# Decoding two edge counts per 16 bit word, and moving one strip's node update into layer 1

## The chip, the cores and the metric

The kernel runs on one core of a Trainium2 chip. The metric is the device time in microseconds of one execution of the whole program; lower is better. Times inside an execution come from a profile of one execution on the chip, counted from the start of its span. The engines are called PE or TensorE (matrix products), DVE or VectorE (elementwise), ACT or ScalarE (activation functions and copies), POOL or GpSimd (small elementwise work) and SP (which only issues transfers here).

## The reference

Two graph layers over 3327 nodes with 64 features and a sparse 0/1 adjacency matrix, each behind a layer norm and a relu, each with a residual addition:

```python
# layer 0: h = relu(layernorm(x)); x = x + L0(h, adj)
left, right = x_t @ w_att[:D, 0], x_t @ w_att[D:, 0]        # x_t = logmap0(h)
adj_att = sigmoid(left[:, None] + right[None, :] + b_att) * adj
x_local = logmap(h[:, None, :], h[None, :, :], c)           # all pairs of nodes
support_t = einsum('ij,ijd->id', adj_att, x_local)
x = x + proj(expmap(h, support_t, c), c)
# layer 1: h = relu(layernorm(x)); x = x + L1(h, adj)
support = h @ weight
rank = cumsum(adj != 0, axis=1); deg = rank[:, -1:]
k = minimum(deg, 100); pos = rank - (deg - k)
w = (adj != 0) * where(pos > 0, 0.5 ** (k - pos), 0)
x = x + w @ support + bias
```

So an edge's weight in layer 1 is two to the power of minus the number of edges behind it in its row, and zero from the hundredth on. Layer 1 needs, for every pair of nodes, a small count; layer 0 reads the same adjacency matrix, so the counts are made there.

## The kernel before, in words

The 3327 nodes are padded to 26 blocks of 128 (`NP` = 3328). The input matrix is given transposed. Layer 0 goes over four **strips** of output nodes (`STRIPS`: blocks 0 to 7, 8 to 15, 16 to 21, 22 to 25), called strips 0 to 3 here; strip 2 is the second but last and strip 3 the last. Each strip goes over all 26 blocks of neighbours in **rounds** (one block in strips 0 to 2, two in the last). A round loads a piece of the matrix, makes a mask (L620), the pairwise products on TensorE (L670, L671), two gelu activations (L857, L858), the attention factor (L653), two combining operations on DVE (L658, L663), and adds to a sum in PSUM (L680, `total`).

In every round a matmul with a triangular matrix counts edges into PSUM (`count`, L631 and L632), and `read` takes the counts out, on ScalarE (L642) or on DVE (L644, L646) by a fixed share (`ON_ACT`). The count is written as one byte into `behind_lo` or `behind_hi`. It is made so that the byte is what the exponent of a bf16 number needs: multiplied by 128, that is shifted by seven bits, it is the bit pattern of the weight. For the blocks 12 to 15 (`JD`) `read` multiplies at once and writes 16 bit weights (`weight_of`); for the other blocks the byte is multiplied in layer 1 (`decode`, L1285 on ScalarE and L1287 on DVE, in turn: 11 each).

After each strip its sum is copied out (`strip_out`, L1157), transposed (`turn`, L1165) and handed to the **node update** (`post`): a long chain of small operations per node which ends in the new x (`x_sb`, L1126 and L1128), its layer norm (L1131 to L1144) and `s2`, the relu of it as two fp16 parts (L1147, L1149). For strips 0 to 2 (`hidden`) its small operations run on POOL and its large ones on DVE; for the last strip all run on DVE, except that the inverse square root is taken with a power on POOL (L1044 with `nhalf`). `post` is a generator: `yield` numbers are prices, and the loop around it (`advance`) lets it run for a certain sum of prices per round (`PORTIONS`) or per block of layer 1 (`LAST` = 8). `LATER` ends a turn, `ACT` asks for an operation of ScalarE, which is issued at the next turn (`asked_of_act`). When several stages are in the list `stages`, they share a turn's sum, the first in the list first. `after(time)` spreads the small operations: it waits ceil(time / `ROUND[k + 1]`) turns for a hidden strip.

The order of PE, DVE and ScalarE instructions is as written (`IN_ORDER`); POOL's order comes from the scheduler. POOL's last operations are, in this order: strip 2's small ones, the addition of the bias to strip 2's part of x (L1304, 128x384), strip 2's root for the layer norm, then three powers for the last strip with one more bias addition (128x256) among them.

**Layer 1** goes over the neighbour blocks in the order `JD` first, then 0 to 11, then 16 to 21, and last 22 to 25, whose `s2` come last. It keeps `LEAD` = 4 blocks decoded ahead in seven buffers `wt`. For each block TensorE adds seven matmuls (L1299), one for each chunk of 512 output columns (the last has 256), into seven PSUM tiles `pw`:

```python
for i, j in enumerate(order):
    for jn in every[: i + 1 + LEAD]:
        if jn not in weights:
            weights[jn] = decode(jn)
    asked_of_act()
    advance(LAST)
    for n in range(len(chunks)):
        add(j, weights[j], n)
```

The last four blocks are then added chunk by chunk. After each chunk its tile is copied out (L1342 on DVE, L1340 on ScalarE), multiplied by the weight matrix (L1328), added to x (L1330) and stored (L1332).

Of the kernel before, what the change touches and what calls it, by code (L numbers as in the profile page):

```python
# [22 lines left out]
P = 128  # L23
# [14 lines left out]

PORTIONS, LAST = (2, 4, 4, 8), 8
BIG, LATER, ACT = 4, 99, 100  # L40
ROUND = (3.5, 3.5, 2.8, 1.9)

LEAD = 4

GSTRIPS = [(0, 7), (7, 7), (14, 6), (20, 6)]
GFMAX = 7 * P
# [35 lines left out]
def halves(n):  # L82
    return [(a, min(a + 512, n)) for a in range(0, n, 512)]
# [363 lines left out]
def fast(ctx, tc, x, adj_t, r, w_att, b_att, weight, bias, out, flag):  # L447
# [76 lines left out]
    def wide(t, n):  # L524
        return t[:, :, None].to_broadcast([P, n, D])
# [96 lines left out]
    def count(n, j):  # L622
# [9 lines left out]
            T.matmul(S.pc[:, f0:f1], cb, now[:, f0:f1], start=S.first, stop=True, skip_group_check=True)  # L632
        S.before, S.first = now, False

    def read(n, j, on_act=None):
        k, lo, hi = rounds[n]
        S = strips[k]
        kept = behind(j)[:, S.i0 : S.i0 + S.F]
        num, den = ON_ACT[k]
        i = NB - 1 - j  # L640
        if on_act or (on_act is None and i * num // den != (i + 1) * num // den):
            A.activation(kept, S.pc[:, : S.F], AF.Relu, scale=128.0 if j in JD else 1.0)  # L642
        elif j in JD:
# [284 lines left out]
    def last_of_ahead():  # L928

        V.tensor_scalar(balm, bal, MIN_NORM, None, op0=ALU.max)  # L930
        V.reciprocal(sk, balm)
        yield
        G.tensor_scalar(w2s, w2, 2.0**27 / HS, None, op0=ALU.mult)
        G.tensor_scalar(ih, babs, 2 / WA, None, op0=ALU.mult)
        G.tensor_mul(su, nrm, balm)
        G.tensor_mul(sv, bal, su)
        G.tensor_scalar(sk, sk, sqc, None, op0=ALU.mult)
        G.tensor_scalar(maxnorm, absr, 1.0 - EPS_BALL, None, op0=ALU.mult)
        G.tensor_mul(c2_c, c_c, c_c)
        G.tensor_scalar(m2c, c_c, -2.0, None, op0=ALU.mult)  # L940
        G.tensor_scalar(p2c, c_c, 2.0, None, op0=ALU.mult)
        ahead.close()

        behind_of["lo"] = ctx.enter_context(tc.tile_pool(name="lo", bufs=1, side="right", reuse_waits="tile")).tile(
            [P, JD.start, NP], U8, name="behind_lo")
        yield


    def range_steps():
        t1 = post_pool.tile([P, NB], F32, name="st1")  # L950
        V.tensor_mul(t1, nrm, node)
# [40 lines left out]
    def post(agg, k):  # L992
# [48 lines left out]
        def after(time):  # L1041

            for do, args, kwargs in asked_of_w:
                do(*args, **kwargs)  # L1044
# [123 lines left out]
    def per_node(k, pa):  # L1168
        nb = STRIPS[k][1]
        agg = post_pool.tile([P, nb, D + 1], F32, name="agg_last" if k + 1 == len(STRIPS) else "agg")  # L1170
        for c in range(0, nb, 4):
            m = min(4, nb - c)
            to, of = agg[:, c : c + m], pa[:, c * P : c * P + m * (D + 1)].rearrange("p (b d) -> p b d", b=m)
            if c == 0:
                V.tensor_copy(to, of)
            else:
                A.copy(to, of)
        return post(agg, k)
# [5 lines left out]
    def advance(portions):  # L1184
        for stage in stages:
            while portions > 0 and not stage.asked:
                portion = next(stage.portions, LATER)
                stage.asked = portion == ACT
                if portion >= LATER:
                    break  # L1190
                portions -= portion
# [78 lines left out]

    late = STRIPS[-1][0]
    order = [*JD, *range(JD.start), *range(JD.stop, late)]
    chunks = halves(NP)
    with tc.tile_pool(name="l1", bufs=2, reuse_waits="tile") as l1, tc.manual_schedule(engines=IN_ORDER):
        decoded = 0

        def decode(j):

            nonlocal decoded
            if j in JD:  # L1280
                return behind(j)
            wt = l1.tile([P, NP], U16, name="wt", bufs=7)
            decoded += 1
            if decoded % 2:
                A.activation(wt, behind(j), AF.Copy, scale=128.0)  # L1285
            else:
                V.tensor_scalar(wt, behind(j), 128.0, None, op0=ALU.mult)  # L1287
# [7 lines left out]
        pw = [l1_ps.tile([P, f1 - f0], F32, name=f"pw{n}") for n, (f0, f1) in enumerate(chunks)]  # L1295

        def add(j, wt, n):
            f0, f1 = chunks[n]
            T.matmul(pw[n], s2[:, j].rearrange("p c d -> p (c d)"), wt[:, f0:f1].bitcast(BF16),  # L1299
                     start=j == order[0], stop=j == NB - 1)  # L1300

        def bias(b0, nb):
            xb = x_sb[:, b0 : b0 + nb]
            G.tensor_add(xb, xb, bias_b[:, None, :].to_broadcast([P, nb, D]))  # L1304
# [4 lines that stand above are left out]
                    weights[jn] = decode(jn)  # L1309
            asked_of_act()  # L1310
            advance(LAST)
            for n in range(len(chunks)):
                add(j, weights[j], n)
            if i % 4 == 3 and i < STRIPS[-2][0]:
                bias(i - 3, 4)
        finish()
        bias(STRIPS[-2][0], late - STRIPS[-2][0])
        bias(late, NB - late)
        for j in range(late, NB):
            if j not in weights:  # L1320
                weights[j] = decode(j)
        ow = [l1.tile([P, 512], F32, name="ow", bufs=4)[:, : f1 - f0] for f0, f1 in chunks]

        def close(n):
            f0, f1 = chunks[n]
            b0, nb = f0 // P, (f1 - f0) // P
            for b in range(nb):
                T.matmul(pw[n][:, b * D : (b + 1) * D], ow[n][:, b * P : (b + 1) * P], w2s, start=True, stop=True)  # L1328
            o = l1.tile([P, 4, D], F32, name="o", bufs=4)
            V.tensor_add(o[:, :nb], pw[n][:, : nb * D].rearrange("p (b d) -> p b d", d=D), x_sb[:, b0 : b0 + nb])  # L1330
            full = nb if b0 + nb < NB else nb - 1
            nc.sync.dma_start(out[f0 : f0 + full * P, :].rearrange("(b p) d -> p b d", p=P), o[:, :full])  # L1332
            if full < nb:
                nc.scalar.dma_start(out[f0 + full * P : N, :], o[: N - f0 - full * P, full])
# [12 lines left out]


@with_exitstack
# [49 lines left out]
```

## Time and profile before

| | |
|---|---|
| median of 3 runs | 418.17 us (416.35 to 418.49) |
| profiled execution, its own time | 418.25 us |
| profiled execution, span | 416.4 us |
| busy PE, DVE, ACT, POOL | 361.1, 373.1, 364.8, 124.0 us |
| last GELU of layer 0 ends (L858) | 354.89 us |
| sum of the last strip copied out (agg_last, L1175) | 360.46 us |
| last strip's s done (L1149) | 395.04 us |
| first matmul with all late blocks decoded (L1299) | 396.89 us |

The table's clock times are of the profiled execution, counted from the start of the span. A row of a profile names the line, the engine, the operation, the tile written and the tiles read, with partitions x elements and type. Busy time is how long an engine had an instruction running; idle time before an instruction is given with what released it. In the chain of waits each step is followed back from the last instruction to what it waited for.

### The profile page before, as it was taken

What the parts mean: (1) busy time and instruction counts of PE and PEld (TensorE: products, weight loads), DVE (VectorE), ACT (ScalarE), POOL (GpSimd) and SP (SyncE); (2) the same over time, 40 slices, a digit from 0 to 9 for tenths busy, and PEclk for the clock granted to TensorE, in tenths of its full rate; (3) what the DMA queues carried; (4) which work ended last, traced back from release to release, by engine and by line L of the source; (5) the groups of instructions that cost most, each with busy time, mean ns of one, the idle gap of its engine ahead of it and who ended that gap; (6) DMA issues with size and microseconds to landing.
All of it is one profiled execution on the core that took longest, in us unless ns stands there. A gap on an engine that the chain in (4) does not pass through costs nothing.

```text
span 416.4 us, 4699 instructions
## 1 busy us (share of the span) xinstructions
PE 361.1 (87%) x1436; PEld 154.4 (37%) x1460; DVE 373.1 (90%) x546; ACT 364.8 (88%) x411; POOL 124.0 (30%) x240
## 2 busy tenths in 40 slices
PE   0088999999997999999997999999777999899793
PEld 0063333333333333333333444444332333344352
DVE  4999799999999899999999798899989899898841
ACT  3589999999998899999999899999996999788810
POOL 8154200000000263930250163801405183452400
PEclk9998999999999899999999899999898999999987
DMA  7315544545466534554437255454643420000012
GB/s 218 123 40 143 161 148 147 158 145 161 146 186 181 152 107 148 153 151 109 145 113 178 94 153 151 119 146 128 186 117 104 114 87 0 2 0 0 2 25 65
DMA packets 23298, 48.99 MB, mean 118 GB/s; under 512 B 8789, under 2 KB 9245, under 8 KB 23265
## 3 DMA queue, kind: packets, MB, share of 16 engines
q1 hardware_dynamic: 20993, 47.66, 39.2%
q10 hardware_dynamic: 1808, 0.46, 0.6%
q0 software_dynamic: 464, 0.49, 0.5%
q8 instruction: 13, 0.21, 0.2%
q14 instruction: 20, 0.16, 0.1%
HBM read 46.40 MB, written 0.87 MB: 114 GB/s over the span
## 4 chain that ended last, share of the span: by engine, by line
DVE 33%; ACT 27%; PE 24%; issue 10%; POOL 3%; DMA 1%; DVEq 0%; POOLq 0%; ACTq 0%
DVE sg L663 9%; PE po L680 9%; ACT sg L653 8%; DVE sg L658 8%; ACT pq L857 8%; ACT pq L858 3%; DVE wt L1287 3%; PE pq L670 3%; PE pq L671 3%; DVE behind_lo L646 3%; PE pc L632 2%; PE pc L631 2%; ACT behind_lo L642 2%; ACT behind_hi L642 2%; PE pw L1299 2%
## 5 line engine op out<-in xcount | busy, mean ns | idle before, releaser
L680 PE MATMUL po<-sg,hw 128*65 128x512 f32 (+1 forms) x364 | 164.5, 576 | 0.5 <-DVE st L972 0.4
L663 DVE SCALAR_TENSOR_TENSOR sg<-pq,sg 128x1024 f32<-128x1024 f32 (+1 forms) x91 | 103.4, 1137 | 6.7 <-ACT pq L858 5.9
L658 DVE SCALAR_TENSOR_TENSOR sg<-sg,ad 128x1024 f32<-128x1024 f32 (+1 forms) x91 | 103.8, 1141 | 0.3
L653 ACT ACTIVATE sg<-left_b,right 128x1024 f32<-128x1024 f32 (+2 forms) x103 | 99.5, 979 | 0.0
L857 ACT ACTIVATE pq<-pq 128x1024 f32<-128x1024 f32 (+1 forms) x91 | 87.1, 957 | 3.5 <-PE pq L671 3.2
L858 ACT ACTIVATE pq<-pq 128x1024 f32<-128x1024 f32 (+1 forms) x91 | 86.2, 947 | 2.9
L680 PEld LDWEIGHTS po<-sg,hw 128*65 128x65 f32 x364 | 50.4, 141 | 71.3 <-issue 57.5
L631 PE MATMUL pc<-mask,ca 128*128 128x512 bf16 (+1 forms) x170 | 62.1, 365 | 11.1 <-DVE behind_hi L646 3.9
L670 PE MATMUL pq<-iu,ju 71*128 71x512 f16 (+1 forms) x182 | 68.2, 375 | 2.4 <-ACT jz L794 1.0
L671 PE MATMUL pq<-iz,jz 128*128 128x512 f16 (+1 forms) x182 | 67.2, 376 | 0.0
L632 PE MATMUL pc<-mask,cb 128*128 128x512 bf16 (+1 forms) x168 | 60.1, 368 | 2.2 <-ACT behind_lo L642 1.7
L620 DVE TENSOR_SCALAR mask<-ad 128x1024 bf16<-128x1024 f32 (+1 forms) x91 | 58.6, 645 | 0.0
L1044 POOL TENSOR_TENSOR dots<-dots,ih 128x8 f32<-128x8 f32 (+1 forms) x3 | 2.2, 720 | 134.3 <-DVE dots L1064 134.3
L1299 PE MATMUL pw<-wt,s 128*128 128x512 bf16 (+1 forms) x150 | 33.6, 374 | 4.3 <-DVE s L1149 2.2
L632 PEld LDWEIGHTS <-cb 128*128 128x128 bf16 x182 | 17.9, 98 | 51.7 <-issue 39.8
L631 PEld LDWEIGHTS <-ca 128*128 128x128 bf16 x175 | 17.3, 99 | 29.9 <-issue 17.8
L670 PEld LDWEIGHTS <-ju 71*128 71x128 f16 x182 | 18.1, 99 | 24.2 <-DVE sg L663 5.8
L1299 PEld LDWEIGHTS <-s 128*128 128x128 f16 x182 | 18.0, 100 | 23.6 <-issue 4.2
L642 ACT ACTIVATE behind_hi<-pc 128x1024 uint8<-128x1024 f32 (+2 forms) x25 | 21.8, 872 | 5.3 <-remote 3.3
L671 PEld LDWEIGHTS <-jz 128*128 128x128 f16 x182 | 18.2, 100 | 19.7 <-issue 3.3
L1304 POOL TENSOR_TENSOR x_sb<-x_sb,bias_b 128x256 f32<-128x256 f32 (+1 forms) x6 | 9.9, 1657 | 51.6 <-DVE w L1133 46.0
L642 ACT ACTIVATE behind_lo<-pc 128x1024 uint8<-128x1024 f32 (+2 forms) x29 | 24.9, 859 | 0.0
(313 smaller groups left out, 369.0 us busy)
## 6 DMA issues: line engine op xcount, KB each, us to landing
ad<-in_adj_t SPq DMA_DIRECT2D x65, 512.0 KB, 3.7
ad<-in_adj_t SPq DMA_DIRECT2D x26, 384.0 KB, 3.2
out<-o SPq DMA_DIRECT2D x6, 128.0 KB, 1.9
left_b<-left_d SPq DMA_DIRECT2D x1, 512.0 KB, 4.6
x_sb<-in_x ACTq DMA_DIRECT2D x1, 416.0 KB, 5.6
x_sb<-in_x SPq DMA_DIRECT2D x1, 416.0 KB
left_b<-left_d SPq DMA_DIRECT2D x1, 384.0 KB
jz<-iz POOLq DMA_DIRECT2D x2, 128.0 KB, 2.6
```

Of the source, the lines that this page charges most:

```text
L631: T.matmul(S.pc[:, f0:f1], ca, S.before[:, f0:f1], start=False, stop=True, skip_group_check=True)
L632: T.matmul(S.pc[:, f0:f1], cb, now[:, f0:f1], start=S.first, stop=True, skip_group_check=True)
L642: A.activation(kept, S.pc[:, : S.F], AF.Relu, scale=128.0 if j in JD else 1.0)
L653: A.activation(part(n, sg, j), S.left[:, : S.F], AF.Tanh, bias=right[:, j : j + 1], scale=0.5)
L658: V.scalar_tensor_tensor(sg, sg, 1.0, ad_of.pop(n)[:, :w], op0=ALU.add, op1=ALU.mult)
L663: V.scalar_tensor_tensor(sg, pq_of.pop(n)[:, :w], WD, sg, op0=ALU.add, op1=ALU.mult)
L670: T.matmul(part(n, pq, j, f0, f1), ju[:KB, j, :], S.iu[:, f0:f1], start=True, stop=False)
L671: T.matmul(part(n, pq, j, f0, f1), jz[:, j, :], S.iz[:, f0:f1], start=False, stop=True)
L680: T.matmul(S.po[: D + 1, f0:f1], hw[:, j, :], part(n, sg_of[n], j, f0, f1), start=j == NB - 1, stop=j == 0)
L857: A.activation(pq, pq, AF.Gelu, scale=-WG / QS)
L858: A.activation(pq, pq, AF.Gelu, scale=WH)
L1299: T.matmul(pw[n], s2[:, j].rearrange("p c d -> p (c d)"), wt[:, f0:f1].bitcast(BF16), start=j == order[0], stop=j == NB - 1)
```

## The change

Five things change together.

1. In layer 1 `decode` writes its weights **by parity**: the 1664 even columns first, then the 1664 odd ones. On DVE it takes two bytes as one 16 bit word: one operation keeps the low byte and shifts it left by seven, one keeps the high byte and shifts it right by one. On ScalarE it is still one activation, which reads every second byte. The two engines still decode in turn.
2. `read` writes the 16 bit weights of blocks 12 to 15 by parity too, so it reads every second word of the PSUM tile.
3. The chunks of layer 1 are now (q, r): the 512 even or odd columns of 1024; the last 256 columns stay together. The copies of the tiles put even and odd columns back in order in a tile of 1024, and the closing operations run for two tiles at a time.
4. The update of strip 2 stops ahead of its change of x until layer 1 has begun (the list `tail` is then filled). Its six operations of 128x384 (new x and the centred x of the layer norm) are issued there, in the first turns, ahead of the last strip's. It is finished at the latest when its own block is due.
5. In layer 1 `after` counts turns of 1.5 us instead of 1.9; the six microseconds that remain for strip 2 are four turns with either.

The core of the diff:

```diff
-ROUND = (3.5, 3.5, 2.8, 1.9)
+ROUND, STEP = (3.5, 3.5, 2.8, 1.9), 1.5
+ACT_DECODES = 2
...
+    def by_parity(t):
+        return t.rearrange("p (r k) -> p r k", r=2)
     def read(n, j, on_act=None):
...
+        of = S.pc[:, : S.F]
+        if j in JD:
+            kept = by_parity(weight_of[:, j - JD.start])[:, :, S.i0 // 2 : (S.i0 + S.F) // 2]
+            of = of.rearrange("p (k r) -> p r k", r=2)
         if on_act or (on_act is None and i * num // den != (i + 1) * num // den):
-            A.activation(kept, S.pc[:, : S.F], AF.Relu, scale=128.0 if j in JD else 1.0)
+            A.activation(kept, of, AF.Relu, scale=128.0 if j in JD else 1.0)
         elif j in JD:
-            V.tensor_scalar(kept, S.pc[:, : S.F], 0.0, 128.0, op0=ALU.max, op1=ALU.mult)
+            V.tensor_scalar(kept, of, 0.0, 128.0, op0=ALU.max, op1=ALU.mult)
...
-                yield from [LATER] * math.ceil(time / ROUND[k + 1])
+                yield from [LATER] * math.ceil(time / (STEP if tail else ROUND[k + 1]))
...
         yield from after(16)
+        while k + 2 == len(STRIPS) and not tail:
+            yield LATER
         V.tensor_mul(w, hs, wide(of_end[:, 0], nb))
...
-    def finish():
-        for stage in stages:
-            for _ in stage.portions:
+    def finish(left=0):
+        while len(stages) > left:
+            for _ in stages.pop(0).portions:
                 pass
-        stages.clear()
...
-    chunks = halves(NP)
+    chunks = [(q, r) for q in range(3) for r in range(2)] + [(3, None)]
+    widths = [512] * 6 + [256]
...
-            if decoded % 2:
-                A.activation(wt, behind(j), AF.Copy, scale=128.0)
+            to = by_parity(wt)
+            if decoded % ACT_DECODES == 1:
+                A.activation(to, behind(j).rearrange("p (k r) -> p r k", r=2), AF.Copy, scale=128.0)
             else:
-                V.tensor_scalar(wt, behind(j), 128.0, None, op0=ALU.mult)
+                pairs_of = behind(j).bitcast(U16)
+                V.tensor_scalar(to[:, 0], pairs_of, 0xFF, 7, op0=ALU.bitwise_and, op1=ALU.logical_shift_left)
+                V.tensor_scalar(to[:, 1], pairs_of, 0xFF00, 1, op0=ALU.bitwise_and, op1=ALU.logical_shift_right)
             return wt
...
+        tail.append(True)
         stages.append(Stage(per_node(len(STRIPS) - 1, pa)))
...
         def add(j, wt, n):
-            f0, f1 = chunks[n]
-            T.matmul(pw[n], s2[:, j].rearrange("p c d -> p (c d)"), wt[:, f0:f1].bitcast(BF16),
+            q, r = chunks[n]
+            w = by_parity(wt.bitcast(BF16))[:, :, 512 * q : min(512 * q + 512, NP // 2)]
+            T.matmul(pw[n], s2[:, j].rearrange("p c d -> p (c d)"), w if r is None else w[:, r],
                      start=j == order[0], stop=j == NB - 1)
...
             advance(LAST)
+            if j == STRIPS[-2][0]:
+                finish(1)
...
+        def copied(n):
+            q, r = chunks[n]
+            to = kept_of[q].rearrange("p (k r) -> p r k", r=2)
+            if r is None:
+                V.tensor_copy(to, by_parity(pw[n]))
+            elif r == 0:
+                V.tensor_copy(to[:, 0], pw[n])
+            else:
+                A.copy(to[:, 1], pw[n])
...
         for n in range(len(chunks)):
             for j in range(late, NB):
                 add(j, weights[j], n)
-            if n % 2:
-                A.copy(ow[n], pw[n])
-            else:
-                V.tensor_copy(ow[n], pw[n])
-            if n > 1:
-                close(n - 2)
-        close(len(chunks) - 2)
-        close(len(chunks) - 1)
+            copied(n)
+            if n > 0 and n % 2 == 0:
+                close(n // 2 - 1)
+        close(3)
```

More of the change, by code (lines that the diff above doesn't have):

```diff
@@ L1197, in asked_of_act @@
                 stage.asked = False
-    def finish():
-        for stage in stages:
-            for _ in stage.portions:
+    def finish(left=0):
+        while len(stages) > left:
+            for _ in stages.pop(0).portions:
                 pass
-        stages.clear()
+    tail = []
     stages, rest_of_ahead = [Stage(range_steps())], last_of_ahead()
@@ L1294, in fast @@
         l1_ps = ctx.enter_context(tc.tile_pool(name="l1_ps", bufs=1, space=PSUM, reuse_waits="tile"))
-        pw = [l1_ps.tile([P, f1 - f0], F32, name=f"pw{n}") for n, (f0, f1) in enumerate(chunks)]
+        pw = [l1_ps.tile([P, f], F32, name=f"pw{n}") for n, f in enumerate(widths)]
         def add(j, wt, n):
-            f0, f1 = chunks[n]
-            T.matmul(pw[n], s2[:, j].rearrange("p c d -> p (c d)"), wt[:, f0:f1].bitcast(BF16),
+            q, r = chunks[n]
+            w = by_parity(wt.bitcast(BF16))[:, :, 512 * q : min(512 * q + 512, NP // 2)]
+            T.matmul(pw[n], s2[:, j].rearrange("p c d -> p (c d)"), w if r is None else w[:, r],
                      start=j == order[0], stop=j == NB - 1)
@@ L1321, in fast, with close @@
                 weights[j] = decode(j)
[L1322 to L1334, printed above, removed]
+        kept_of = [l1.tile([P, min(NP - 1024 * q, 1024)], F32, name="ow" if q < 3 else "ow_last", bufs=2 if q < 3 else 1)
+                   for q in range(4)]
+        def copied(n):
[7 more added lines that the diff above has]
+                A.copy(to[:, 1], pw[n])
+        def close(q):
+            for h in range(0, 8 if q < 3 else 2, 4):
+                b0 = 8 * q + h
+                nb = min(4, NB - b0)
+                pc = pw[2 * q + h // 4]
+                for b in range(nb):
+                    T.matmul(pc[:, b * D : (b + 1) * D], kept_of[q][:, (h + b) * P : (h + b + 1) * P], w2s, start=True, stop=True)
+                o = l1.tile([P, 4, D], F32, name="o", bufs=4)
+                V.tensor_add(o[:, :nb], pc[:, : nb * D].rearrange("p (b d) -> p b d", d=D), x_sb[:, b0 : b0 + nb])
+                full = nb if b0 + nb < NB else nb - 1
+                f0 = b0 * P
+                nc.sync.dma_start(out[f0 : f0 + full * P, :].rearrange("(b p) d -> p b d", p=P), o[:, :full])
+                if full < nb:
+                    nc.scalar.dma_start(out[f0 + full * P : N, :], o[: N - f0 - full * P, full])
         for n in range(len(chunks)):
```

## The prediction, made before the change ran

> **What bounds the kernel now.** I read the page's busy shares, then the stretches of the end, the chain of waits, and last the timeline there. The busy shares (engine, us, share of the span, instructions):
>
> ```profile
> PE 361.1 (87%) x1436; PEld 154.4 (37%) x1460; DVE 373.1 (90%) x546; ACT 364.8 (88%) x411; POOL 124.0 (30%) x240
> ```
>
> Three engines stand within 3% of each other, so a gain on one alone is worth only the gap to the next. The change touches the last 60 us, so these count. Stretches (us; busy us and instructions of PE, PEld, DVE, ACT, POOL; TensorE clock; DMA):
>
> ```profile
> 361.00:366.00 5.00, 5.00 (x27) 2.46 (x26) 4.90 (x14) 5.00 (x3) 4.24 (x5) 1.00 0.01 3
> 381.00:386.00 5.00, 3.92 (x20) 1.85 (x19) 4.60 (x12) 2.26 (x1) 0.13 (x1) 1.00 0.00 0
> 391.00:397.00 6.00, 2.94 (x13) 1.19 (x13) 5.02 (x8) 5.03 (x3) 0.65 (x1) 1.00 0.00 0
> 397.00:403.00 6.00, 6.00 (x29) 3.75 (x28) 1.81 (x3) 1.17 (x2) 0.00 (x0) 0.72 0.01 2
> ```
>
> Layer 1 starts with TensorE full; towards its end TensorE starves (2.94 of 6.00) while DVE stays busy. The chain of waits (start, us, engine, tile, line) says for what:
>
> ```profile
> 389.52 2.14 POOL rn_last L1044
> ...
> 392.90 1.80 DVE wt L1287
> 394.70 0.33 DVE s L1149
> 395.04 1.81 DVE wt L1287
> 396.85 0.04 issue
> 396.89 3.47 PE pw L1299 x9
> ```
>
> The end is set by the last strip's node update: some fifty small DVE instructions from agg_last (360.46) to its s (L1149, done at 395.04), with three POOL powers and DVE's decodes (wt, L1287) queued between them; one more decode follows before TensorE can finish its first chunk (396.89). The prices (groups by shape; the numbers after the bar are total us and mean ns):
>
> ```profile
> L1287 DVE TENSOR_SCALAR wt<-behind_lo 128x3328 uint16<-128x3328 uint8 x6 | 11.3, 1890 | 0.1
> L620 DVE TENSOR_SCALAR mask<-ad 128x1024 bf16<-128x1024 f32 x65 | 44.3, 682 | 0.0
> L620 DVE TENSOR_SCALAR mask<-ad 128x768 bf16<-128x768 f32 x26 | 14.3, 551 | 0.0
> L1285 ACT ACTIVATE wt<-behind_lo 128x3328 uint16<-128x3328 uint8 x6 | 17.6, 2963 | 0.0
> ```
>
> From the two masks, 256 elements cost 131 ns: 0.512 ns each over a fixed 158 ns. 3328 elements then give 1862 ns, so the decode runs at that same rate. And the timeline, at the end of the strips and on POOL:
>
> ```profile
> 353.88 1.01 ACT L858 ACTIVATE pq<-pq 128x1024 f32<-128x1024 f32 x1
> 354.62 2.10 POOL L1304 TENSOR_TENSOR x_sb<-x_sb,bias_b 128x384 f32<-128x384 f32 x1 [6.30 <-DVE w L1133]
> 355.96 1.23 DVE L663 SCALAR_TENSOR_TENSOR sg<-pq,sg 128x1024 f32<-128x1024 f32 x1
> 360.46 0.43 DVE L1175 COPY agg_last<-po 128x260 f32<-128x260 f32 x1 [0.56 <-PE po L1165]
> 365.04 0.23 POOL L1044 TENSOR_TENSOR rt<-rt,t 128x6 f32<-128x6 f32 x1
> 365.36 1.72 POOL L1044 TENSOR_SCALAR rt<-rt 128x6 f32<-128x6 f32 x1
> ```
>
> The reader is to see that the last gelu ends at 354.89 and L663 starts 1.07 us later, and that a POOL operation of 0.2 us takes 1.72 us while a DVE decode runs (365.12 to 367.02).
>
> **What the Trainium skill says.** "VectorE: DVE Perf Modes", The perf-mode tier table: tensor_scalar does two elements per cycle on fp32 in SBUF and four on 16 bit. The first agrees with 0.512 ns per element; no 16 bit case is large enough here to show the second. "GPSIMD Engine Reference", Specifications: GpSimd shares its SBUF interfaces with VectorE and contends with its two-port modes. The 1.72 us agrees. "SBUF — State Buffer", Door 1: SBUF is read in lines of 16 bytes, so a step of two bytes is free, while PSUM lines hold two fp32 values. The trace shows neither at length: only L870 reads PSUM with a step of two, 0.15 us for 8 elements and 0.15 us for 2, which excludes nothing.
>
> **The change part by part.**
>
> 1. *End of the strips.* Six 128x384 DVE operations of strip 2 (L1122 to L1133) leave. From start to start they take 0.93 (348.54 to 349.47), 1.06 (351.21) and 1.05 (353.40): 3.0 us. ScalarE has no gap there, and its last gelu still ends at 354.89, so L663 moves from 355.96 to about 354.95. Gain 1.0 of the 3.0: sums, turn and agg_last move to 359.4.
>
> 2. *DVE decode.* One operation of 3328 becomes two of 1664, on 16 bit words. At four per cycle (half of 0.512): 158 + 426 = 584 ns, start to start about 0.50 (successors overlap by 0.08), so 1.0 per decode against 1.82: 0.8 saved, eleven times. A power that waits behind a decode on POOL is released 0.8 sooner too. The trace excludes neither two nor one per cycle; I take four because the skill's table says it for this operation, and keep two (1.93 per decode) and one (1890 ns each, 3.6) as rivals.
>
> 3. *The moved update.* It is now first in the list of stages, so it goes ahead of the last strip: six operations (3.1 us) and two decodes before w_last. POOL issues in the old order, and there the bias addition on x_sb (L1304) stands before strip 2's root, and that before the last strip's first power. The bias addition waits for the moved w, done at 363.9 instead of 354.5. Laying the instructions in the new order with the trace's durations: bias done 366.1, root from 366.3 to 371.5 (before: 367.7), the power at 372.4. So rt_last starts at about 372.4 instead of 370.47: two microseconds **later**, though it started a microsecond earlier. Behind strip 2's waiting w (L1144) and rt_last on DVE stands the tenth decode; it ends at 374.3, and TensorE reaches its block at 377.2, so that wait starves nobody. ScalarE's s cast waits 1.6, and strip 2's s is due at 385.5 only.
>
> 4. *The rest of the chain.* From rt_last to s it was 24.6 us with seven decodes. Seven times 0.8 saves 5.6. ScalarE takes some back, because its decodes of 2.96 stand in front of k_last (about 0.9) and of the square u_last (0.5), POOL and small waits 0.5. Left 3.7: s done at 393.3. No decode follows s now (the eleventh goes before it) and ScalarE's last decode ends at 391. TensorE starts its late blocks at 393.4, chunk 0 is whole at 394.3 against 397.3: 3.0. The same laying out of the old order ends 1.0 late, so the true gain lies between 3.0 and 4.0; I take **3.3**. TensorE does not bind: 22 blocks of 1.39 (six of 0.213, one of 0.107) from 359.2 end at 389.7.
>
> 5. *ScalarE decode*, input with a step of two bytes: taken as unchanged, 2.96. Less is excluded (same element count); at most each element costs double, 0.84 more.
>
> 6. *Reads of rows 12 to 15* (16 of them, 7424 elements on ScalarE, 5888 on DVE) now read PSUM with a step of two. Taken as 0. Less than nothing is excluded, since it is as many elements. At most each takes a second cycle: 6.2 us on ScalarE and 6.1 on DVE, in different rounds, so up to 12.
>
> 7. *Tail.* Copies write fp32 with a step of two, closings come in pairs; ten small closing matmuls follow the last chunk as before. The last pair waits for ScalarE's copy of chunk 5 (L1340, 0.59) over chunk 6's four matmuls (0.43): 0.16, and as much again for the step: +0.3 (0 to 1.5). SP's and POOL's queues issue the same transfers. TensorE idles 3.7 us before its late blocks; it already runs them at a clock of 0.72.
>
> Sum, against the profiled execution's own 418.25 (span 416.4): 418.25 - 3.3 + 0.3 = 415.25. The median of the three runs is 418.17, 0.08 lower; so 415.2 to 415.3, call it **415.3**.
>
> **The rivals.**
> - *Bit operations at two or one per cycle* (ends slower). Place: the same DVE chain. At 1.93 per decode the chain's s comes near 402, about +5.5: 424.0; at 3.6 it is DVE alone, about +24: 442. It decides from 1.3 us per decode, an operation of 0.73 us. For it: nothing in the trace runs faster than two per cycle. Against: the table.
> - *PSUM reads with a step are slower.* Place: the rounds of rows 12 to 15, where ScalarE and DVE are both full. Half a cycle more per element is 3.1 us on each; with the slack between rounds taken off about +4 together, so 419.3. It turns the gain over from about 0.2 us per read.
> - *ScalarE's decode slows* by its step: 11 times up to 2.8, over 430.
> - *The gain is eaten*: POOL's queue and ScalarE's decodes hold the last strip as long as before; 417 to 418.5.
>
> **How the numbers follow.** A measurement of this kernel tells about 0.5%, 2.1 us, from no change. Likeliest, 0.47: 415.3, own range 413.0 to 417.0, faster in 0.40 and same in 0.07. Gain eaten 0.13: 0.10 same, 0.03 slower. PSUM step 0.15: 0.04 same, 0.11 slower. Bit operations 0.20 (two per cycle 0.10, one 0.10): slower. ScalarE 0.05: slower. Faster 0.40, same 0.21, slower 0.39. The range leaves out one per cycle, ScalarE's case and 0.05 below: 413.0 to 424.5.
>
> **What would show it.** Right: decode operations of 1664 near 0.58 us, agg_last near 359.4, rt_last about 2 us later than before, s near 393, TensorE's late blocks starting on s. Wrong: decode operations of 1.0 or more; weight_of reads above 1014 ns (ScalarE) or 1219 ns (DVE); ScalarE decodes above 2.96; agg_last not earlier.

## The result, and the profile after

The changed kernel takes 412.36 us (median of 13 runs, 411.08 to 415.36) against 417.55 us for the kernel before in the same series (13 runs): a ratio of 0.9879, 95% interval 0.9853 to 0.9905. (A series is a set of kernels that ran together with the kernel before; a ratio is always taken within its series.) The prediction said 415.3, with a range of 413.0 to 424.5. Faster was right, but by 5.2 us and not by 2.9, and the median lies 0.6 us below the range. The profiled execution's own time is 412.02 us (span 410.3) against 418.25 (span 416.4).

The busy shares of the changed kernel (engine, us, share of the span, instructions):

```profile
PE 356.2 (87%) x1460; PEld 151.0 (37%) x1460; DVE 366.0 (89%) x557; ACT 364.9 (89%) x411; POOL 115.8 (28%) x240
```

DVE and POOL have lost 7 and 8 us; most of the time was won at the end of the kernel. The same four stretches as before (us; busy us and instructions of PE, PEld, DVE, ACT, POOL; TensorE clock; DMA share; GB/s):

```profile
361.00:366.00 5.00, 5.00 (x26) 2.42 (x25) 4.90 (x10) 4.32 (x3) 1.52 (x3) 1.00 0.00 0
381.00:386.00 5.00, 5.00 (x27) 2.45 (x25) 4.42 (x12) 5.00 (x4) 0.53 (x1) 1.00 0.02 3
391.00:397.00 6.00, 6.00 (x38) 3.68 (x36) 2.35 (x5) 1.24 (x2) 0.00 (x0) 1.00 0.17 39
397.00:403.00 6.00, 5.44 (x44) 4.52 (x42) 2.89 (x7) 0.61 (x1) 0.00 (x0) 1.00 0.26 58
```

The changed kernel has its last s some 4.6 us earlier, so its third stretch already lies behind TensorE's wait: TensorE is busy for 6.00 us where it was 2.94, and its clock is 1.00 in both of the last two, where the fourth had 0.72. The groups by shape give the new prices (total us, mean ns, idle ahead):

```profile
L1297 ACT ACTIVATE wt<-behind_lo 128x3328 uint16<-128x3328 uint8 x6 | 17.7, 2968 | 0.4 <-PE pw L1315 0.4
L652 DVE TENSOR_SCALAR weight_of<-pc 128x1024 uint16<-128x1024 f32 x4 | 4.9, 1219 | 0.5 <-PE pc L633 0.5
L650 ACT ACTIVATE weight_of<-pc 128x1024 uint16<-128x1024 f32 x4 | 4.1, 1014 | 0.0
L1301 DVE TENSOR_SCALAR wt<-behind_hi 128x1664 uint16<-128x1664 uint16 x5 | 2.9, 586 | 0.0
L1300 DVE TENSOR_SCALAR wt<-behind_hi 128x1664 uint16<-128x1664 uint16 x5 | 2.9, 585 | 0.0
```

Two bit operations of 0.585 us do what one of 1.89 did (one of the twenty-two took longer, see the last section); ScalarE's decode and the reads of blocks 12 to 15 cost what they cost before. In what follows, rt_last is the first DVE operation behind the last strip's first POOL power, and s is the last operation of its update. And the timeline (start, us, engine, line, operation, idle before and releaser), from the last strip's sum to TensorE's late blocks:

```profile
357.93 0.43 DVE L1185 COPY agg_last<-po 128x260 f32<-128x260 f32 x1 [0.56 <-PE po L1175]
362.61 1.28 POOL L1320 TENSOR_TENSOR x_sb<-x_sb,bias_b 128x384 f32<-128x384 f32 x1 [16.13 <-DVE w L1143]
369.95 1.41 POOL L1052 TENSOR_TENSOR rn_last<-t_last,nhalf 128x4 f32<-128x4 f32 x1
371.39 0.16 DVE L1052 TENSOR_TENSOR rt_last<-rn_last 128x4 f32<-128x4 f32 x1 [0.93 <-POOL rn_last L1052]
374.01 0.22 DVE L1052 SCALAR_TENSOR_TENSOR k_last<-k_last,absr,rn_last 128x4 f32<-128x4 f32 x1 [0.33 <-ACT k_last L1094]
385.87 0.42 DVE L1148 TENSOR_REDUCE t_last<-u_last 128x4 f32<-128x256 f32 x1 [0.48 <-ACT u_last L1146]
390.04 0.42 DVE L1159 TENSOR_TENSOR s<-w_last,s 128x256 f16<-128x256 f32 x1
390.52 2.76 PE L1315 MATMUL pw<-wt,s 128*128 128x512 bf16 x12 [1.73 <-DVE s L1159]
```

For comparison, the first rt_last of the kernel before and the waits of its TensorE ahead of the nine late matmuls:

```profile
370.47 0.15 DVE L1044 TENSOR_TENSOR rt_last<-rn_last 128x4 f32<-128x4 f32 x1
395.10 0.60 PE L1299 MATMUL pw<-wt,s 128*128 128x512 bf16 x2 [2.19 <-DVE s L1149]
396.27 0.38 PE L1299 MATMUL pw<-wt,s 128*128 128x512 bf16 x1 [0.57 <-ACT wt L1285]
396.89 3.47 PE L1299 MATMUL pw<-wt,s 128*128 128x512 bf16 x9 [0.25 <-DVE wt L1287]
```

The last strip's node update still sets the end: TensorE waits for its s. But it waits 1.73 us and not 3.0 in three pieces, the late blocks start on s with every block decoded, and 12 matmuls take 2.76 us (0.23 each) where nine took 3.47.

Part of the 6.1 us between the two profiled executions is not the change. At 231 us DVE's combining operation (L671, L663 before) is 0.36 us earlier than before, at 250 us it is 1.98 us earlier, in code that the change does not touch. The stretch from 228 to 236, first of the kernel before, then of the changed one:

```profile
228.00:236.00 8.00, 7.36 (x32) 3.77 (x33) 5.72 (x9) 6.75 (x10) 0.00 (x0) 0.79 0.49 143
```

```profile
228.00:236.00 8.00, 7.73 (x41) 4.08 (x42) 7.39 (x12) 7.91 (x13) 0.00 (x0) 1.00 0.46 138
```

TensorE's clock was cut there in one execution and not in the other (0.79 against 1.00). By 340 us this has given 1.83 us to the changed kernel. The 6.1 us are these 1.83, and at the end of the kernel: end of the strips 0.70, agg_last to s 2.05, s to the first chunk's copy 1.14, the tail (from that copy to the last addition's end) 0.76, less 0.35 behind the last addition.

### The profile page after: what moved, and what is told of

It is laid out like the page before. It is cut to its first block, busy times and chain, and to the rows that moved or that the text cites. A ratio compares the mean times of both kernels' runs of the same rounds, so it can differ in the third digit from the quotient of the medians.

```text
span 410.3 us, 4738 instructions
## 1 busy us (share of the span) xinstructions
PE 356.2 (87%) x1460; PEld 151.0 (37%) x1460; DVE 366.0 (89%) x557; ACT 364.9 (89%) x411; POOL 115.8 (28%) x240
## 4 chain that ended last, share of the span: by engine, by line
DVE 33%; ACT 28%; PE 26%; issue 10%; DMA 1%; POOL 0%; POOLq 0%; DVEq 0%; ACTq 0%
DVE sg L671 11%; DVE sg L666 10%; PE po L688 8%; ACT sg L661 8%; ACT pq L865 7%; PE pw L1315 7%; ACT pq L866 3%; DVE behind_lo L654 3%; ACT behind_lo L650 2%; PE pq L678 2%; PE pq L679 2%; PE pc L632 2%; PE pc L633 2%; DVE behind_hi L654 2%; PE pw L1359 1%
## 5 line engine op out<-in xcount | busy, mean ns | idle before, releaser
L688 PE MATMUL po<-sg,hw 128*65 128x512 f32 (+1 forms) x364 | 161.8, 568 | 0.0
L671 DVE SCALAR_TENSOR_TENSOR sg<-pq,sg 128x1024 f32<-128x1024 f32 (+1 forms) x91 | 103.7, 1139 | 7.2 <-ACT pq L866 6.7
L632 PE MATMUL pc<-mask,ca 128*128 128x512 bf16 (+1 forms) x175 | 64.2, 367 | 12.1 <-DVE behind_hi L654 4.0
L688 PEld LDWEIGHTS po<-sg,hw 128*65 128x65 f32 x364 | 49.3, 138 | 68.6 <-issue 55.7
L678 PE MATMUL pq<-iu,ju 71*128 71x512 f16 (+1 forms) x182 | 67.2, 369 | 1.7 <-ACT jz L802 0.8
L633 PE MATMUL pc<-mask,cb 128*128 128x512 bf16 (+1 forms) x182 | 65.3, 369 | 2.7 <-ACT behind_lo L650 1.7
L679 PE MATMUL pq<-iz,jz 128*128 128x512 f16 (+1 forms) x182 | 65.6, 368 | 0.0
L1315 PE MATMUL pw<-wt,s 128*128 128x512 bf16 (+1 forms) x154 | 31.6, 364 | 1.7 <-DVE s L1159 1.7
L632 PEld LDWEIGHTS <-ca 128*128 128x128 bf16 x175 | 17.3, 99 | 30.9 <-issue 18.8
L1320 POOL TENSOR_TENSOR x_sb<-x_sb,bias_b 128x256 f32<-128x256 f32 (+1 forms) x6 | 7.5, 1259 | 61.6 <-DVE w L1143 55.9
```

The costliest lines, as they stand in the source:

```text
L632: T.matmul(S.pc[:, f0:f1], ca, S.before[:, f0:f1], start=False, stop=True, skip_group_check=True)
L671: V.scalar_tensor_tensor(sg, pq_of.pop(n)[:, :w], WD, sg, op0=ALU.add, op1=ALU.mult)
L678: T.matmul(part(n, pq, j, f0, f1), ju[:KB, j, :], S.iu[:, f0:f1], start=True, stop=False)
L679: T.matmul(part(n, pq, j, f0, f1), jz[:, j, :], S.iz[:, f0:f1], start=False, stop=True)
L688: T.matmul(S.po[: D + 1, f0:f1], hw[:, j, :], part(n, sg_of[n], j, f0, f1), start=j == NB - 1, stop=j == 0)
L1315: T.matmul(pw[n], s2[:, j].rearrange("p c d -> p (c d)"), w if r is None else w[:, r], start=j == order[0], stop=j == NB - 1)
```

## The experiments

Theory A: the speed of the decode is the gain; the moved update wins about 1 us at the strips' end and pays more than that by standing ahead of the last strip. Rivals: the move pays (B), or the layout does (C). Theory D, which came from the clock of 0.72: a long wait of TensorE for s also costs clock when the late blocks start, so a shorter wait is paid twice. Its rival E: the clock comes and goes by itself.

**Without the move.**

```diff
-        while k + 2 == len(STRIPS) and not tail:
-            yield LATER
```

> The changed kernel with the second but last strip's update left in layer 0 (the loop that held it back is taken out; decode, parity layout and closing by pairs stay). Theory A (the decode's speed is the gain; the move buys 0.7 to 1.0 us at the strips' end and pays 3.4 between agg_last and rt_last): agg_last 0.7 to 1.0 us later than in the changed kernel, rt_last starts about 10 us after agg_last and not 13.5, s done 2 to 2.5 us earlier; time 1.5 to 2.5 us under the changed kernel, about 7 under the kernel before. Rival B (the move is what pays, because less stands ahead of agg_last, and the later rt_last is hidden by TensorE's 22 blocks): s comes earlier but TensorE's blocks now end last, starting 0.7 to 1.0 later; time equal to the changed kernel or up to 1 us above it, 4 to 5 under the kernel before.

Measured: 410.66 us (ratio 0.9841, 0.9803 to 0.9879). agg_last at 359.34, rt_last 7.52 later. The timeline of TensorE and of s in this kernel:

```profile
364.75 28.03 PE L1313 MATMUL pw<-wt,s 128*128 128x512 bf16 x138
387.16 0.43 DVE L1157 TENSOR_TENSOR s<-w_last,s 128x256 f16<-128x256 f32 x1 [1.78 <-ACT s L1155]
```

TensorE never waits: 138 matmuls in one piece run from blocks that need no strip 3 into the late ones. s is done 2.9 us earlier than in the changed kernel (agg_last to s 28.3 us, there 32.5), and most of that buys nothing, because TensorE is now the bound. So the move looks like a loss, of 1.7 us by the medians and of 1.2 between the profiles once the differences of layer 0 (0.72 us) are taken off; A expected 1.5 to 2.5. The chain shows why: 7.5 us from agg_last to rt_last (A had 10) against 13.5. The two kernels ran in different series and the intervals of their ratios overlap, so the sign rests on the traces and on the repetition below.

**The move alone**, on the kernel before (the `tail` list, the loop that holds strip 2's update back, and `finish(1)`; old decode, layout and closing).

> The kernel before with the move alone (the second but last strip's update held back into layer 1 and finished ahead of the last strip; old decode, old layout, old closing). Theory A: agg_last 0.7 to 1.0 us earlier, rt_last 13 to 13.5 us after it (10.0 before), s done 2 to 3 us later; time 2 to 3 us over the kernel before. Rival B (the move pays by itself): 1 to 2 us under the kernel before.

Measured: 424.48 us, ratio 1.0170 (1.0133 to 1.0207): slower by 7.3 us, about three times what A said. agg_last came early as expected, but rt_last came 17.3 us after it and not 13 to 13.5. POOL shows why, and TensorE what follows:

```profile
362.94 2.58 POOL L1308 TENSOR_TENSOR x_sb<-x_sb,bias_b 128x384 f32<-128x384 f32 x1 [16.93 <-DVE w L1135]
367.08 2.96 POOL L1044 TENSOR_TENSOR rn<-t,nhalf 128x6 f32<-128x6 f32 x1
370.68 1.95 POOL L1044 TENSOR_SCALAR rt<-rt 128x6 f32<-128x6 f32 x1
```

```profile
389.53 2.97 PE L1303 MATMUL pw<-wt,s 128*128 128x512 bf16 x14 [1.41 <-DVE wt L1290]
400.41 4.65 PE L1303 MATMUL pw<-wt,s 128*128 128x512 bf16 x12 [5.94 <-DVE s L1151]
```

These POOL operations, which run beside decodes of 1.89 us, are stretched (the same three take 1.28, 1.65 and 0.20 us in the changed kernel), and with six more operations in the queue DVE delivers decoded blocks too late as well. The move's price depends on the decode: it is a bad change alone and at most a small loss behind a fast decode.

**The changed kernel with a slow decode.**

```diff
-                pairs_of = behind(j).bitcast(U16)
-                V.tensor_scalar(to[:, 0], pairs_of, 0xFF, 7, op0=ALU.bitwise_and, op1=ALU.logical_shift_left)
-                V.tensor_scalar(to[:, 1], pairs_of, 0xFF00, 1, op0=ALU.bitwise_and, op1=ALU.logical_shift_right)
+                V.tensor_scalar(to, behind(j).rearrange("p (k r) -> p r k", r=2), 128.0, None, op0=ALU.mult)
```

> The changed kernel with VectorE's decode done as one multiply from every second byte into the parity layout, with everything else (layout, move, pairs) kept. Theory A (four elements per cycle on 16 bit words is the gain): one decode 1.85 to 1.9 us in place of 2 times 0.585, s done 5 to 7 us later than in the changed kernel, time 1 to 4 us over the kernel before. Rival C (the gain lies in the layout, the move or the closing, not in the speed of the decode): within 1.5 us of the changed kernel, 4 or more under the kernel before.

Measured: 425.73 us, ratio 1.0207 (1.0165 to 1.0249). One decode takes 1.886 us. So 0.8 us on each of eleven decodes, 9 us of DVE, are worth 13.4 us of the kernel. That is 8.5 us over the kernel before, where A had 1 to 4; it allowed about 9 in all. Part of the rest is clock (TensorE waits 5.94 us for s, and the late matmuls then take 4.75 us and not 2.76), part is in the powers. The last strip's second power, in this kernel and then in the changed one:

```profile
383.56 0.17 DVE L1052 TENSOR_SCALAR y_last<-y_last 128x4 f32<-128x4 f32 x1
383.63 1.89 DVE L1299 TENSOR_SCALAR wt<-behind_hi 128x3328 uint16<-128x3328 uint8 x1
383.81 2.58 POOL L1052 TENSOR_TENSOR rn_last<-y_last,nhalf 128x4 f32<-128x4 f32 x1 [8.67 <-DVE y_last L1052]
386.42 0.16 DVE L1052 TENSOR_TENSOR rt_last<-rn_last 128x4 f32<-128x4 f32 x1 [0.90 <-POOL rn_last L1052]
```

```profile
378.23 0.17 DVE L1052 TENSOR_SCALAR y_last<-y_last 128x4 f32<-128x4 f32 x1
378.31 0.58 DVE L1300 TENSOR_SCALAR wt<-behind_hi 128x1664 uint16<-128x1664 uint16 x1
378.48 1.28 POOL L1052 TENSOR_TENSOR rn_last<-y_last,nhalf 128x4 f32<-128x4 f32 x1 [7.12 <-DVE y_last L1052]
378.81 0.58 DVE L1301 TENSOR_SCALAR wt<-behind_hi 128x1664 uint16<-128x1664 uint16 x1
379.79 0.16 DVE L1052 TENSOR_TENSOR rt_last<-rn_last 128x4 f32<-128x4 f32 x1 [0.39 <-POOL rn_last L1052]
```

From y_last to rt_last it is 2.86 us with the slow decode and 1.56 with the pair: 1.30 saved where the decode itself saves 0.8. A decode with a power behind it is worth 0.5 more than a decode alone. From rt_last to the last s there are seven decodes and two such powers: 7 x 0.8 + 2 x 0.5 = 6.6 us, measured 6.54 (25.19 against 18.65 between the starts of the two). Another 3.84 us lie between agg_last and rt_last (17.30 against 13.46), with four decodes and POOL's bias and root among them.

**The kernel before with TensorE kept busy** while it waits for s: nine matmuls that nothing reads, ahead of the late blocks.

```diff
+        warm = l1_ps.tile([P, 512], F32, name="warm")
...
+        for _ in range(9):
+            T.matmul(warm, cb, weight_of[:, 0, :512].bitcast(BF16), start=True, stop=True)
         for n in range(len(chunks)):
```

> The kernel before with nine added matmuls of 128x512, into a spare tile that nothing reads, just ahead of the late blocks: they fill TensorE's idle time while it waits for s. Theory D (the halved clock in the tail of the kernel before, 0.72 in 397 to 403, comes from that idle time, so a shorter wait for s also wins the tail's clock): clock 1.00 from 397 to 403, late matmuls 0.23 us each in place of 0.39, time 1 to 1.7 us under the kernel before. Rival E (the halvings come by themselves, or the added work brings them): clock in the tail as before, time within 0.7 us of the kernel before, or above it.

Measured: 415.44 us, ratio 0.9963 (0.9941 to 0.9985), faster though it does more. The stretch of the tail:

```profile
397.00:403.00 6.00, 6.00 (x44) 4.63 (x42) 2.66 (x5) 1.15 (x3) 0.00 (x0) 1.00 0.19 44
```

The clock is 1.00 where it was 0.72, and the nine late matmuls ahead of this stretch take 2.10 us where they took 3.47. Theory D holds here: by the ratio it is worth 1.5 us.

**The changed kernel once more, and three variants of it beside it.**

> The changed kernel once more, beside the three that follow. In its profile: s done near 390.5 less whatever clock windows layer 0 has, TensorE waits 1.7 us for s, late matmuls at a clock of 1.00. Time 412 to 413, clock over the span 0.98 to 0.983 in the mean. If TensorE's halved windows in layer 0 differ from run to run, the start of layer 1 (agg_last 357.93 in the first profile) moves by up to 2 us in steps of 0.7 to 1.7.

Measured: 411.77 us (ratio 0.9896, 0.9850 to 0.9942), 0.2 under what was expected. The wait for s is 1.73 us and the clock behind it 1.00 again; agg_last is at 356.92. By 340 us this execution is another 1.0 us ahead of the first, in layer 0 alone.

The last strip first: the last strip's stage stands ahead of strip 2's for three blocks, then behind it.

```diff
-        stages.append(Stage(per_node(len(STRIPS) - 1, pa)))
+        stages.insert(0, Stage(per_node(len(STRIPS) - 1, pa)))
...
+            if i == 3:
+                stages.reverse()
             advance(LAST)
```

> The changed kernel with the last strip's stage put ahead of the moved update for the first three blocks of layer 1, and behind it after that; so the last strip's first power stands before the moved strip's bias and root on POOL. Theory A (the move's price is that it stands ahead of the last strip; its gain is the earlier agg_last): agg_last as in the changed kernel, rt_last 7.5 to 9 us after it and not 13.5, the moved strip's s before TensorE needs it (about 22 us after agg_last), TensorE without a wait for s; time about 0.7 us under the kernel without the move (410.66), so 409.5 to 411, and 2 to 2.5 us under the changed kernel. Rival F (the six operations cost the last strip 3 us wherever they stand, and now the moved strip's s comes late too): 411.5 to 413, the same as the changed kernel, with TensorE waiting for s as before or at the moved strip's first row.

Measured: 414.60 us, ratio 0.9939 (0.9917 to 0.9961), over 2 us slower than the changed kernel by the medians; the intervals of the two ratios just overlap. rt_last comes 10.4 us after agg_last (A had 7.5 to 9), 3 us sooner than there. The six operations of 128x384 now stand further down in the same DVE queue, and yet the last w_last, from which s is made, is done 29.7 us after agg_last (31.2 there). That gain is lost on ScalarE: it is busy with two decodes and starts its cast to s 2.4 us after w_last is done (0.04 there). So s comes 32.9 us after agg_last (32.5 there), with a wait of 1.78 for ScalarE ahead of it:

```profile
390.98 0.42 DVE L1154 SCALAR_TENSOR_TENSOR w_last<-w_last,rn_last 128x256 f32<-128x256 f32 x1
393.77 0.39 ACT L1157 CAST s<-w_last 128x256 f16<-128x256 f32 x1
394.19 0.43 DVE L1159 TENSOR_TENSOR s<-w_last,s 128x256 f16<-128x256 f32 x1 [1.78 <-ACT s L1157]
394.67 4.01 PE L1315 MATMUL pw<-wt,s 128*128 128x512 bf16 x12 [2.13 <-DVE s L1159]
```

Neither theory named this: A left out ScalarE's decodes, and by rival F the six operations would cost the last strip 3 us wherever they stand; the time lies above F's range too. Part of the difference is clock: the wait is 0.4 us longer, and the 12 late matmuls take 4.01 us in place of 2.76. So A's account of the move is incomplete: what counts is all that stands ahead of s in both queues, DVE's and ScalarE's, not only what stands ahead of the first power.

s later, without and with a busy TensorE: seven operations on w_last that change nothing; then the same with sixteen matmuls that nothing reads ahead of the late blocks.

```diff
         V.scalar_tensor_tensor(w, w, 0.0, wide(rn, nb), op0=ALU.max, op1=ALU.mult)
+        if k + 1 == len(STRIPS):
+            for _ in range(7):
+                V.tensor_scalar(w, w, 0.0, None, op0=ALU.max)
```

> The changed kernel with seven added operations on w_last (128x256, each a maximum with zero that changes nothing) ahead of the cast to s: s comes 2.0 to 2.5 us later, and TensorE waits 3.7 to 4.2 us in place of 1.7. Theory D (a wait of that length halves TensorE's clock when the late blocks start): clock in the 6 us after the wait 0.6 to 0.75, time 3.5 to 4.2 us over the changed kernel, clock over the span 0.004 lower. Rival E (the halving does not come from the wait): clock 1.00 there, time 2.0 to 2.5 us over the changed kernel.

> The kernel with the seven added operations on w_last, and with sixteen added matmuls of 128x512 into a spare tile that nothing reads, just ahead of the late blocks, so that TensorE is busy for 3.7 of the about 4 us. Theory D: clock 1.00 after the wait, time 2.0 to 2.6 us over the changed kernel, 1.3 to 1.8 under the kernel with the added operations alone. Rival E: the same time as that kernel or above it, by up to 0.3.

Measured: 416.73 us (ratio 0.9994, 0.9963 to 1.0026) without, 415.07 (0.9957, 0.9932 to 0.9981) with the busy TensorE. First the stretch around the wait without the busy TensorE, then the late matmuls with it:

```profile
391.00:397.00 6.00, 3.98 (x10) 1.49 (x11) 2.62 (x6) 0.75 (x2) 0.00 (x0) 0.54 0.00 0
```

```profile
396.85 2.76 PE L1319 MATMUL pw<-wt,s 128*128 128x512 bf16 x12 [0.56 <-DVE s L1162]
```

A wait that is 2.3 us longer (4.03 in place of 1.73) costs 5.0 us by the medians, more than D's 4.2; the 12 late matmuls account for 2.5 of them (5.30 us in place of 2.76). With TensorE busy through the wait it is 1.7 less (3.3). D is shown from both sides: in the kernel before by taking the idle time away, in the changed one by bringing it back. That the second difference is 3.3 and not 2.3 stays open. The mean granted clock of its 22 runs was 0.978, and 0.981 in the six runs of the changed kernel, so cuts in layer 0 may hold the rest; that is not shown.

**A part of the move**: the four operations that make the new x stay in layer 0; only the mean and the subtraction (two operations) are held back.

> The changed kernel with only the end of the second but last strip's update held back into layer 1: the products with the weights and the two additions on x_sb (four operations of 0.55 us) stay in layer 0, the mean and the subtraction (two operations, 1.1 us) move. Theory A (1.07 us at the strips' end is all that the move can win, and what it costs is what it puts ahead of the last strip): agg_last as early as in the changed kernel (13.0 us or less over the last gelu's end would be the same as there), rt_last 9 to 11 us after it and not 13.5, s early enough that TensorE waits 0 to 0.5 us; time 409.5 to 411. Rival G (the four operations left there still hold up the strips' end, and POOL's bias and root hold the last strip all the same): agg_last as in the kernel without the move, rt_last 12 us or more after it; 411 to 413.

Measured: 411.09 us (ratio 0.9873, 0.9839 to 0.9907). agg_last is as early as with the whole move (357.94 and 357.93, with the same start of L671 at 341.8), so those two are all that the strips' end gains from. rt_last comes 10.4 us after agg_last. ScalarE again starts its cast 2.4 us after w_last is done, s waits 1.78 us for it, and TensorE still waits 0.82 us, more than A's 0.5:

```profile
389.61 2.76 PE L1315 MATMUL pw<-wt,s 128*128 128x512 bf16 x12 [0.82 <-DVE s L1159]
```

**Layout and closing alone** (slow decode from the parity layout, no move).

> The kernel before with the parity layout and the closing by pairs alone (VectorE's decode is one multiply from every second byte, as slow as before; no move). Theory A (layout and closing cost about 1 us in the tail and 0 elsewhere, the decode's speed is the whole gain): decodes 1.89 us, weight_of reads 1014 and 1219 ns as before, time 0 to 1.5 us over the kernel before. Rival C (the layout brings part of the gain): 1 us or more under the kernel before.

Measured: 418.16 us against 416.07 in its series, ratio 1.0054 (1.0033 to 1.0075). The decodes take 1.89 us and the reads 1014 and 1223 ns, so the tail is left: from the first late matmul of a whole chunk to the last addition's end it is 13.45 us, in the kernel before 12.66, with a cut clock in both. That is 0.8 of the 2.1, and 2.1 is more than A's 1.5. The rest is not accounted for; the mean granted clock of these 16 runs was 0.974, and 0.978 in the kernel before beside them, which would fit more cuts of the clock in layer 0; that, and why there were more, is not shown. The layout and the closing are a cost, not a gain.

**Without the move, again**, in that series.

> The changed kernel without the move once more, in the same call as the kernel with a part of the move: 410 to 411.5, TensorE without a wait for s (0.3 us at most), clock over the span 0.98 or above.

Measured: 410.49 us (ratio 0.9854, 0.9825 to 0.9883), again with no wait for s. The kernel without the move had the lowest medians of all, 410.66 and 410.49, against 412.36 and 411.77 for the whole change and 411.09 for a part of the move. The ratios to the kernel before, 0.9841 and 0.9854 against 0.9879 and 0.9896, say the same, but the whole change never ran in one series with it and the intervals overlap: that the move is a loss is likely and not certain.

## Why the prediction was right or wrong

- *End of the strips: right at its place, 0.3 too much at the end.* L671 starts 1.09 us earlier once layer 0's 1.83 us are taken off. TensorE's last sums took 0.4 longer, and agg_last gained 0.70, not 1.0.
- *DVE decode: right.* 585 ns against 584. Per element that is half the time of the masks, which fits the four elements per cycle that the Trainium skill ("VectorE: DVE Perf Modes", The perf-mode tier table) gives tensor_scalar on bf16; here it is two bit operations on uint16. The rivals of one and two per cycle fall.
- *Moved update: right in mechanism, 0.5 short from agg_last on.* 13.46 us from agg_last to rt_last against 13.0 predicted and 10.01 before; POOL took the bias, then the root, then the first power, as told.
- *Rest of the chain: wrong.* The step that failed is "ScalarE takes some back ... POOL and small waits 0.5". This term was mis-sized, and in part had the wrong sign: I took 1.9 off the 5.6 that seven decodes save. DVE's two waits for ScalarE measured 0.33 and 0.48 (the second is no more than u_last's own 0.42 and the hand-over), where I had 0.9 and 0.5. On POOL the sign was wrong: each power behind a decode saved 0.5 more, not less (from the operation ahead of the power to rt_last 2.86 to 1.56 and 2.95 to 1.57 us). rt_last to s saved 5.5 us (24.57 to 19.07), not 3.7. It is not the 6.5 of the slow decode, because the moved strip's s (L1159) now stands between rt_last and k_last, and the small waits come on top: about 1.0. In the clock of the profile before, s is done at 392.3 where I had 393.3.
- *No decode after s, TensorE starts on it: right.* From s to the first copy it is 1.13 us; I had 1.0.
- *ScalarE's decode and the reads with a step of two: right.* 2960 to 2968 ns against 2963; 1219 and 1014 ns as before. For ScalarE's decode the reason was the Trainium skill's "SBUF — State Buffer", Door 1, by which a step of two bytes within a line of 16 is free; the trace agrees. For the reads the page gave no such reason, since its PSUM lines hold only two fp32 values: that they cost nothing was an assumption, and it held.
- *Tail: wrong.* The step that failed is the last of it: TensorE "already runs them at a clock of 0.72". I read that clock as given, and so put nothing for it. It was a cost of TensorE's idle time before its late blocks, which is not paid in the two profiles of the changed kernel. The pair closing costs 0.8 (I had 0.3), the clock gives about 1.6 back: -0.76 in place of +0.3. The idle time itself was misread: the trace has 2.19, 0.57 and 0.25 us, 3.0 in all, and not 3.7.
- *The base.* 418.17 of three runs lay high: the later series of the kernel before have medians of 417.55, 417.23, 416.65 and 416.07. Between the profiles, with layer 0 taken off, 4.3 us were won where the sum had 3.0: 3.9 up to the first chunk's copy (I had 3.3) and 0.8 in the tail (I had a loss of 0.3), less 0.35 behind the last addition. The medians differ by 5.2. The 0.9 beyond the 4.3 may be layer 0's clock, and is not shown.
- *The rivals.* None came true. The chance of 0.39 for slower rested on four of them: slower bit operations, PSUM reads, a slower decode on ScalarE, and a chain that gains nothing. The runs show none of the four.

## What to carry to other kernels

When an engine's operations stand in the same queue as a long chain with hand-overs to another engine, price the operation and the hand-over together: a decode that was 0.8 us shorter freed 1.3 us at each of the two places where a POOL power stood behind it. Before taking a cut clock in a stretch as given, ask which idle time stands ahead of it. And an update that is moved off one path lands on another: here it gained 0.7 us and put six operations into the queue that set the end, and the versions without it had the lowest medians. Where two engines share the last steps, count both queues: in two variants ScalarE's decode took back what DVE had won.

## What the runs showed of the hardware that was not expected

- TensorE's clock and its own idle time. The clock is cut to half in stretches of 3.41 us or a multiple of it, and the stretches of one execution lie on a grid: in the kernel before, the cuts at 39.07, 134.64, 230.22, 298.48, 315.55 and 397.47 us start 28, 28, 20, 5 and 24 times 3.413 us apart. So it may not be the length of a wait that counts but how much of it falls into one stretch of the grid. Around the waits for s, first in the kernel before, then in the changed one, then with the last strip first (us; busy us and instructions of PE, PEld, DVE, ACT, POOL; TensorE clock; DMA):

```profile
394.06:397.47 3.41, 1.56 (x6) 0.59 (x7) 2.94 (x4) 2.16 (x1) 0.00 (x0) 1.00 0.00 0
397.47:400.88 3.41, 3.41 (x12) 1.82 (x10) 1.01 (x2) 0.59 (x1) 0.00 (x0) 0.50 0.00 0
388.93:392.35 3.42, 1.83 (x9) 0.89 (x10) 2.22 (x5) 0.41 (x1) 0.00 (x0) 1.00 0.00 0
392.35:395.76 3.41, 3.41 (x25) 2.43 (x24) 1.54 (x3) 0.62 (x1) 0.00 (x0) 1.00 0.02 6
392.62:396.03 3.41, 1.36 (x7) 0.65 (x8) 0.71 (x2) 1.54 (x2) 0.00 (x0) 1.00 0.00 0
396.03:399.44 3.41, 3.41 (x13) 1.92 (x11) 1.10 (x2) 0.62 (x1) 0.00 (x0) 0.50 0.00 0
```

In the profiles of this case, a stretch at full clock around the wait for s was followed by one at half clock where TensorE was busy in it for 1.68 us or less, and not where it was busy for 1.78 us or more. The changed kernel's 1.83 is close to that, so an execution in which the grid lies otherwise may be cut; no profile shows one, and waits of one length at two places of the grid were not tried. In layer 0 it is not that simple: the cut at 39.07 followed a stretch with 2.10 us busy. The 12 late matmuls took 2.76 us behind waits of 0.82 and 1.73, and 4.01, 5.30 and 4.65 us behind waits of 2.13, 4.03 and 5.94. Each of these is one profiled execution.
- VectorE and GpSimd hold each other up in both directions. The Trainium skill's "GPSIMD Engine Reference", Specifications, says that the two share their SBUF interfaces and contend when VectorE runs in a two-port mode; here a DVE operation of 0.58 us took 1.39 beside POOL's bias addition of 1.28 us (362.61 to 363.89):

```profile
362.95 1.39 DVE L1301 TENSOR_SCALAR wt<-behind_lo 128x1664 uint16<-128x1664 uint16 x1
```

That is the one case in eleven decodes.
